# Graph layers 1 to 3 of a four-layer network: the round's order of steps rewritten

## The chip, the cores and the metric

The kernel runs on one core of one Trainium2 chip. The metric is the device time of one execution in microseconds (us). Before the change it is 3620.76 us, the median of three runs (3611.67 to 3627.42). Five engines of the core are named as in the profile: PE is TensorE (PEld its weight loads), DVE is VectorE, ACT is ScalarE, POOL is GpSimd, SP is SyncE, which here only issues transfers.

## The reference

The input is a batch of 64 graphs with 256 nodes and 256 features each (`x`), and a weighted adjacency matrix `adj` for each graph. Four layers follow one another; each is a graph network with a residual sum and a layer norm:

```python
x = _layernorm(x + L0(x, adj))   # a recurrence over the 256 nodes
x = _layernorm(x + L1(x, adj))   # relu(norm_adj @ (x W^T + b))
x = _layernorm(x + L2(x, adj))   # attention, one head of 256, masked by adj
x = _layernorm(x + L3(x, adj))   # attention, 8 heads of 32, masked by adj > 0
```

Layer 0 runs over the nodes for all graphs at once. Layers 1 to 3 treat each graph by itself:

```python
# layer 1
norm_adj = adj_matrix * d_inv_sqrt[:, :, None] * d_inv_sqrt[:, None, :]
output = relu(einsum('bnm,bmo->bno', norm_adj, x @ W.T + b))
# layer 2
att = softmax(scores * mask - NEG * (1.0 - mask))
out = relu((att @ v) @ Wo + bo)
# layer 3, in each of 8 heads of width 32
attn = softmax(where(adj > 0, q @ k.T / sqrt(32), NEG))
out = concat_heads(attn @ v) @ Wo + bo
```

## The kernel before, in words

`_recurrence` does layer 0 and leaves its result in memory. `_layers` (line 850 on) does layers 1 to 3, and it alone is touched. A third function repeats layer 3 in a safer form if a flag asks for it.

In `_layers` each graph is an object whose methods are the steps: a few instructions on one or more engines. All data are 32-bit floats. A tile of one graph is 128 partitions by 2 halves by 256 elements. The steps that the change moves, or that stand around it:

- `xT(l)` transposes the features before layer l: four transposes on PE into one PSUM bank (helper line 930), then one copy by ACT (line 1021).
- `qk2(s)` is a product (eight matmuls, helper line 940) and two ACT activations (1046). `t`, `g`, `v2`, `w2`, `s2`, `f2`, `qk3`, `v3` and `f3` are products too, read out by ACT or DVE. `f2` is read out by three DVE instructions (1087, 1091).
- `s3(hc)` makes the scores of four heads, the half `hc` of the eight. Sixteen matmuls use 32 rows of the array each (1123), into four banks of their own. Then come four DVE adds of the mask (1130) and four ACT exps (1131).
- `o3(hc)` multiplies these by the values: 16 matmuls into 32 columns each, four heads side by side, and 16 with ones in place of the values, which give the sums (1143). DVE then reads out: a reciprocal (1149), a product (1150) and a maximum for the flag (1151). `f3` is the output product, added to `y` by DVE (1158).
- `norm_a(l)` is the first half of a layer norm: five DVE instructions (905 to 908) and one power on POOL (909). `norm_b(l)` is the second half: one DVE instruction (915) and two ACT activations (917).
- `adT` transposes the adjacency matrix: PE, two ACT activations (1011), one DVE comparison (1016). `degrees_a` and `degrees_b` make its degrees on DVE and POOL.
- `store` sends the result out from SP; `load` fetches the three tiles of a graph, also from SP. `bias_3` sends a copy of `y` to memory from SP and adds a bias on POOL.

Nothing reorders the work: a manual schedule is on, and each engine performs its instructions in the order in which the program issues them. That order is the text `ROUND`, seven lines of steps. Five graphs are in work at once, one for each letter: L is being prepared, A is in layer 1, B in layer 2, C in layer 3 and E at layer 3's end. The loop over `t` runs the text once for each round, preceded by the loads of graph t+2, and a graph moves from one letter to the next: what is C in one round is E in the next. Steps of graphs that don't exist are left out in the first and last rounds.

The products and transposes take turns in four PSUM banks (`bank`, line 922). A step that takes a bank waits until the step four turns before has been read out. The four score banks are separate.

Of the kernel before, what the change touches and what calls it, by code (L numbers as in the profile page):

```python
# [849 lines left out]
def _layers(tc, ident, Hd, Yd, x, adj, w1, b1, l2, l3, out):  # L850
# [9 lines left out]
    B, N, D = x.shape  # L860
# [5 lines left out]
    with ExitStack() as ctx:  # L866
# [98 lines left out]
        class Graph:  # L965
# [197 lines left out]


        ROUND = """
            A.xT.1 E.o3.1 B.xT.2 B.qk2.0 C.norm_b.2
            A.t B.qk2.1 B.v2 L.residual_0 B.masks
            E.f3 C.xT.3 A.g C.bias_3 L.norm_a.0
            C.qk3.0 C.qk3.1 E.norm_a.3 A.norm_a.1 L.norm_b.0 B.s2 B.exp2
            C.s3.0 C.v3 B.w2 L.degrees_a  # L1170
            B.pT2 E.norm_b.3 E.store A.norm_b.1 C.s3.1 B.f2 L.degrees_b
            C.o3.0 L.adT B.norm_a.2
        """.split()
        graphs = [Graph(b) for b in range(B)]
        graphs[0].load()
# [129 lines left out]
@with_exitstack  # L1305
def kernel(ctx: ExitStack, tc: tile.TileContext, ins, out):
    nc = tc.nc
    x, adj = ins["x"], ins["adj"]
    B, N, D = x.shape
    main = ctx.enter_context(tc.tile_pool(name="main", bufs=1))  # L1310
    dram = ctx.enter_context(tc.tile_pool(name="dram", bufs=1, space=bass.MemoryType.DRAM))
    ident = main.tile([P, P], F32, name="ident")
    make_identity(nc, ident)
    Hd = dram.tile([N, B, D], F32, name="Hd")
    _recurrence(
        tc, ident, Hd, x, adj,
        *(ins["L0_gnn_" + n] for n in (
            "W_ioux", "b_ioux", "W_iouh", "b_iouh", "W_coux", "b_coux", "W_couh", "b_couh"
        )),
    )  # L1320
    l2, l3 = (
        {w + n: ins[f"{l}_gnn_{w}{n}"] for w in "Wb" for n in "vkqo"} for l in ("L2", "L3")
    )
    Yd = dram.tile([B, P, 2, D], F32, name="Yd")
    found = _layers(tc, ident, Hd, Yd, x, adj, ins["L1_gnn_W"], ins["L1_gnn_b"], l2, l3, out)
    with tc.If(found > 0):
        _layer_3(tc, ident, Yd, adj, l3, out)
# [36 lines left out]
```

## Time and profile before

| what | us |
|---|---|
| median of three runs | 3620.76 |
| lowest and highest | 3611.67, 3627.42 |
| the profiled execution | 3625.61 |
| its span, first to last instruction | 3623.6 |
| PE busy | 3338.4 (92%) |
| DVE busy | 2374.3 (66%) |
| ACT busy | 1836.0 (51%) |
| POOL busy | 1487.7 (41%) |
| mean granted clock of PE | 0.975 |

The profile is one execution. Busy times overlap, since the engines work side by side, and the chain that ended last says which of them set the end: PE has 74% of it. The recurrence takes the first 1592 us or so; the rounds of layers 1 to 3 follow. In the rounds from 1700 to 3500 us PE is busy some 98% of the time, at a granted clock of 1.00. Four views are used below: the page's slices; the windows, which give each engine's busy time and the granted clock in a stretch; the waits, which give the total, the count and the longest of each kind; and the timeline, where a line is a group of like instructions with its start, its length, engine, source line, operation, and in brackets the idle time before it and what ended that.

### The profile page before, as it was taken

The page shows a single profiled execution, that of the slowest core. Times are in us where ns is not written, and L with a number is a line of the kernel's source. Part 1 is how long each engine was busy: PE and PEld are TensorE (multiplying, and loading weights), DVE is VectorE, ACT ScalarE, POOL GpSimd, SP SyncE. Part 2 cuts the span into 40 slices and gives each one's busy share as a digit, 9 for nine tenths or more (in the row PEclk, how much of TensorE's full clock was granted, in tenths as well). Part 3 has the DMA queues.
Part 4 walks back from the last instruction along what each step waited for, and adds up shares of the span by engine and source line. Part 5 has one row for each costly group of instructions (what it writes and reads, how often), then busy time and mean ns, then how long its engine had stood idle before and what let it go on. Part 6 is the DMA issues. An engine that isn't in the chain of part 4 may idle for free.

```text
span 3623.6 us, 81902 instructions
## 1 busy us (share of the span) xinstructions
PE 3338.4 (92%) x30882; PEld 2384.0 (66%) x30882; DVE 2374.3 (66%) x7052; ACT 1836.0 (51%) x4771; POOL 1487.7 (41%) x1669
## 2 busy tenths in 40 slices
PE   5599999999989998858999999999999999999998
PEld 4455555555555555536777777777777777777776
DVE  2366766766667777734777677666677777776765
ACT  0144444444434444424666666666666666666664
POOL 2266666766556777722222222222222222222221
PEclk9799999999999999978999999999999999999999
DMA  8746566687876563240111111111111111111100
GB/s 279 219 129 142 155 170 154 147 189 201 192 186 167 150 165 106 67 107 29 45 45 45 45 45 45 45 45 45 45 45 45 45 45 44 43 45 45 45 27 22
DMA packets 389637, 348.51 MB, mean 96 GB/s; under 512 B 107244, under 2 KB 355192, under 8 KB 384120
## 3 DMA queue, kind: packets, MB, share of 16 engines
q1 hardware_dynamic: 367280, 323.84, 33.6%
q10 hardware_dynamic: 21960, 19.41, 1.6%
q8 instruction: 245, 4.01, 0.5%
q14 instruction: 152, 1.25, 0.1%
HBM read 224.01 MB, written 99.61 MB: 89 GB/s over the span
## 4 chain that ended last, share of the span: by engine, by line
PE 74%; POOL 6%; DMA 6%; DVE 6%; issue 4%; ACT 3%; SPq 2%; ACTq 0%; DVEq 0%; POOLq 0%
PE mm L940 13%; PE o L1143 7%; PE rc L581 4%; PE rc L589 4%; PE s L1123 4%; PE mm_2f L940 3%; PE mm_3v L940 3%; PE mm_3f L940 3%; PE mm_t L940 3%; PE mm_g L940 3%; PE mm_2s L940 3%; PE mm_2v L940 3%; PE mm_2w L940 3%; PE late L505 3%; PE tr_x L930 3%
## 5 line engine op out<-in xcount | busy, mean ns | idle before, releaser
L614 DVE SCALAR_TENSOR_TENSOR ACC<-keep,S,ACC 128x128 f32<-128x128 f32 x1712 | 504.5, 345 | 191.4 <-ACT hs L632 175.8
L909 POOL TENSOR_TENSOR rstd<-rstd,mhalf 128x2 f32<-128x2 f32 x256 | 173.1, 694 | 627.8 <-DVE rstd L908 626.1
L650 POOL TENSOR_TENSOR ACC<-ACC,far 128x384 f32<-128x384 f32 (+1 forms) x313 | 371.9, 1188 | 24.5
L1130 DVE TENSOR_TENSOR p<-s,neg 128x512 f32<-128x512 f32 x512 | 317.7, 683 | 68.6 <-PE s L1123 68.6
L581 PE MATMUL rc<-WxT,xqT 128*64 128x256 f32 x2048 | 329.8, 401 | 1.8 <-issue 1.8
L917 ACT ACTIVATE y<-y,shift,rstd 128x256 f32<-128x256 f32 x512 | 273.5, 598 | 95.3 <-DVE shift L915 91.0
L1035 POOL TENSOR_TENSOR y<-y,g 128x512 f32<-128x512 f32 x64 | 81.2, 1269 | 565.4 <-issue 556.4
L646 POOL TENSOR_TENSOR far<-hs,S 128x384 f32<-128x384 f32 (+1 forms) x313 | 304.8, 974 | 4.7
L1131 ACT ACTIVATE p<-p 128x512 f32<-128x512 f32 x512 | 295.0, 627 | 2.6 <-DVE p L1130 1.6
L752 POOL TENSOR_TENSOR ready<-ACC,dinv 128x128 f32<-128x128 f32 x255 | 102.3, 401 | 419.0 <-DVE ACC L614 397.9
L905 DVE BATCH_NORM_STATS2 st<-y 128x6 f32<-128x256 f32 x512 | 209.1, 408 | 93.8 <-POOL y L1035 89.0
L1158 DVE TENSOR_TENSOR y<-y,mm_3f 128x512 f32<-128x512 f32 x64 | 44.0, 688 | 281.3 <-PE mm_3f L940 281.3
L1149 DVE RECIPROCAL rT<-o 128x256 f32<-128x256 f32 x128 | 224.1, 1751 | 0.3 <-PE o L1143 0.3
L1046 ACT ACTIVATE qk<-mm,b_cols 128x256 f32<-128x256 f32 x256 | 107.4, 470 | 202.6 <-PE mm L940 202.6
L1021 ACT COPY xT<-tr_x 128x512 f32<-128x512 f32 x192 | 112.4, 587 | 182.7 <-PE tr_x L930 182.7
L589 PE MATMUL rc<-WhT,xpT 128*64 128x128 f32 x2048 | 170.2, 287 | 28.1 <-ACT xpT L598 28.0
L598 ACT COPY xpT<-xpT_ps 128x128 f32<-128x128 f32 x256 | 68.3, 267 | 245.5 <-PE xpT_ps L596 245.5
L589 PEld LDWEIGHTS rc<-WhT,xpT 128*64 128x64 f32 x2048 | 107.7, 137 | 117.8 <-ACT xpT L598 84.1
L807 DVE TENSOR_TENSOR zcc<-zc,rc 128x128 f32<-128x128 f32 x256 | 72.8, 284 | 155.1 <-ACT rc L805 155.1
L581 PE MATMUL z_ps<-WxT,xqT 128*64 128x128 f32 x2048 | 171.0, 289 | 0.0
L940 PE MATMUL mm<-xT,W2q 128*128 128x256 f32 x512 | 129.4, 396 | 44.7 <-ACT xT L1021 44.7
L1098 ACT ACTIVATE qk<-mm,b_cols 128x256 f32<-128x256 f32 x256 | 107.5, 471 | 118.2 <-PE mm L940 118.2
(165 smaller groups left out, 7980.2 us busy)
## 6 DMA issues: line engine op xcount, KB each, us to landing
xX<-in_x_dram ACTq DMA_DIRECT2D x16, 1024.0 KB
Us<-xu SPq DMA_DIRECT2D x64, 256.0 KB
rows<-in_adj_dram SPq DMA_DIRECT2D x64, 256.0 KB
ACC<-Us SPq DMA_DIRECT2D x32, 512.0 KB
xq<-in_x_dram SPq DMA_DIRECT2D x64, 256.0 KB
Hw<-hs SPq DMA_DIRECT2D x512, 32.0 KB
Es<-eu SPq DMA_DIRECT2D x64, 256.0 KB
early_sb<-Es SPq DMA_DIRECT2D x32, 512.0 KB
```

The lines of the kernel that those rows point to most:

```text
L581: nc.tensor.matmul(G[o * B:(o + 1) * B], xqT[a, i // 2][:, i % 2, kc, h * B:(h + 1) * B], WxT[:, kc, o, gates], start=False, stop=False, s ...
L589: nc.tensor.matmul(G[o * B:(o + 1) * B], hT[:, kc * B:(kc + 1) * B], WhT[:, kc, o, g], start=False, stop=(kc == 1), skip_group_check=True,)
L614: nc.vector.scalar_tensor_tensor(acc[:, 0, :], keep[:, j % 2, :], s, acc[:, 0, :], ALU.mult, ALU.add)
L646: nc.gpsimd.tensor_mul(tmp[:, 0:count, :], hs.unsqueeze(1).to_broadcast(shape), s.unsqueeze(2).to_broadcast(shape),)
L650: nc.gpsimd.tensor_add(acc, acc, tmp[:, 0:count, :])
L905: nc.vector.bn_stats(st, y[:, c, :])
L917: nc.scalar.activation(y[:, c, :], y[:, c, :], AF.Identity, bias=shift[:, c:c + 1], scale=rstd[:, c:c + 1],)
L940: nc.tensor.matmul(pm[:, c, :], lhsT[:, k, c * P:(c + 1) * P], rhs[:, k, :], start=(k == 0), stop=(k == 1),)
L1130: nc.vector.tensor_add(p, s_ps[i], self.neg3)
L1131: nc.scalar.activation(p, p, AF.Exp, scale=ISQ)
L1143: nc.tensor.matmul(o_ps[i * HD:(i + 1) * HD, part, :], ones if part else self.v3_sb[:, k, h * HD:(h + 1) * HD], self.ps_of[hc][i][:, k, :] ...
L1149: nc.vector.reciprocal(rT, o_ps[:, 1, :])
```

## The change

Only the text `ROUND` is edited; no instruction is added or taken away.

```diff
         ROUND = """
-            A.xT.1 E.o3.1 B.xT.2 B.qk2.0 C.norm_b.2
+            A.xT.1 B.xT.2 B.qk2.0 C.norm_b.2 E.o3.0 E.o3.1
             A.t B.qk2.1 B.v2 L.residual_0 B.masks
-            E.f3 C.xT.3 A.g C.bias_3 L.norm_a.0
-            C.qk3.0 C.qk3.1 E.norm_a.3 A.norm_a.1 L.norm_b.0 B.s2 B.exp2
-            C.s3.0 C.v3 B.w2 L.degrees_a
-            B.pT2 E.norm_b.3 E.store A.norm_b.1 C.s3.1 B.f2 L.degrees_b
-            C.o3.0 L.adT B.norm_a.2
+            C.xT.3 A.g E.f3 C.bias_3 L.norm_a.0
+            C.qk3.0 C.qk3.1 A.norm_a.1 L.norm_b.0 B.s2 B.exp2
+            C.s3.0 C.v3 B.w2 L.degrees_a E.norm_a.3
+            B.pT2 A.norm_b.1 C.s3.1 B.f2 E.norm_b.3 E.store L.degrees_b
+            L.adT B.norm_a.2
         """.split()
```

`o3` of the first half of the heads leaves the last line of one round (as C) and comes into the first line of the next (as E, the same graph), beside `o3` of the second half. The transposes of layer 2 and its first product go ahead of both. `f3` goes behind `xT.3` and `g`. The last norm's first half goes from the fourth line to the end of the fifth, and its second half and the store from behind `pT2` to behind `f2`.

## The prediction

> **What bounds the kernel now.** First the page's forty slices: they separate the recurrence of layer 0 from the rounds of layers 1 to 3 (from slice 18 on), where alone the diff acts.
>
> ```profile
> PE   5599999999989998858999999999999999999998
> ...
> ACT  0144444444434444424666666666666666666664
> ...
> PEclk9799999999999999978999999999999999999999
> ```
>
> TensorE is busy nine tenths or more through the rounds, at the full granted clock; ScalarE has six tenths. The windows view puts numbers on 500 us of it:
>
> ```profile
> core 0: us, PE busy (x) PEld busy (x) DVE busy (x) ACT busy (x) POOL busy (x), PEclk, DMA share, GB/s
> ...
> 2500.00:3000.00 500.00, 489.16 (x3467) 386.83 (x3466) 346.69 (x932) 304.43 (x655) 127.69 (x149) 1.00 0.14 44
> ```
>
> PE 98%, VectorE 69%, ScalarE 61%. The add of g into y (L1035) starts at 2599.39 and, one round later, at 2629.82: a round takes 30.43 us and PE's own order sets it. The averages would let VectorE and ScalarE wait or hurry freely, so the question is what happens at the seam between two rounds. The waits view, 1700 to 3500 us, shows the largest wait of PE and two waits of the others near the seam:
>
> ```profile
> DVE p L1130 <- PE s L1123: 54.7, 59, 0.9
> ...
> PE mm L940 <- ACT xT L1021: 39.8, 59, 0.7
> ACT adT L1011 <- PE tr_ad L930: 30.4, 60, 1.2
> ```
>
> Then the timeline across a seam (start, length of the merged group), ordered by time:
>
> ```profile
> 2608.65 1.15 PE L1123 MATMUL s<-qk,qk 32*128 32x256 f32 x16
> ...
> 2609.55 2.08 ACT L917 ACTIVATE y<-y,shift,rstd 128x256 f32<-128x256 f32 x4
> ...
> 2609.73 1.99 PE L940 MATMUL mm_2f<-w,pT 128*128 128x256 f32 x8
> ...
> 2609.82 2.48 DVE L1130 TENSOR_TENSOR p<-s,neg 128x512 f32<-128x512 f32 x4 [0.93 <-PE s L1123]
> ...
> 2611.53 2.19 ACT L1131 ACTIVATE p<-p 128x512 f32<-128x512 f32 x4
> ...
> 2611.65 1.07 PE L1143 MATMUL o<-p,v 128*32 128x256 f32 x16
> ...
> 2612.22 0.87 DVE L1087 SCALAR_TENSOR_TENSOR f<-mm_2f,sums,b2o_r 128x256 f32<-128x256 f32 x2
> ...
> 2614.21 0.84 ACT L1011 ACTIVATE adT<-tr_ad,dis 128x256 f32<-128x256 f32 x2 [0.50 <-PE tr_ad L930]
> ...
> 2617.10 0.59 ACT L1021 COPY xT<-tr_x 128x512 f32<-128x512 f32 x1 [1.57 <-PE tr_x L930]
> ...
> 2617.74 1.99 PE L940 MATMUL mm<-xT,W2q 128*128 128x256 f32 x8 [0.68 <-ACT xT L1021]
> ```
>
> The reader is to see that ScalarE works without a break from before 2608 to 2613.72, behind PE, and that PE fills that stretch and the next with the two four-wide products (o3, L1143: 2611.65 to 2613.52 and 2614.54 to 2616.41). They are the cover under which ScalarE catches up.
>
> [...] all four norm_b activations sit before the exps at 2611.53, as emitted. [...]every stretch of half clock that can be read lasts a multiple of 3.41 us[...] a product takes 1.72 us from start to start, f2 before the four-wide one 1.92.
>
> The tail of this trace shows what a gap does: 3.11 us of PE waiting, then half clock (stretch, its length, PE busy, granted clock, then DMA).
>
> ```profile
> 3586.00:3587.50 1.50, 0.67 (x2) 1.00 0.00 0
> 3587.50:3589.00 1.50, 0.00 (x0) 1.00 0.00 0
> 3589.00:3590.50 1.50, 0.09 (x1) 0.57 0.00 0
> ...
> 3598.00:3599.50 1.50, 1.50 (x5) 0.52 0.00 0
> ```
>
> ```profile
> 3594.87 3.78 PE L940 MATMUL mm<-xT,W3q 128*128 128x256 f32 x8 [0.68 <-ACT xT L1021]
> ```
>
> The same eight matmuls take 3.78 us there and 1.99 at 2617.74: half clock doubles them.
>
> **The change, part by part**, walked through the seam with the clock of the old trace. Up to s3.1's matmuls (2608.65) PE has the same work.
>
> - *E.norm_a.3 moved behind degrees_a.* Five VectorE instructions (0.43, 0.18, 0.40, 0.18, 0.17 us; 1.3 from first to next) and one pow on POOL, whose queue is idle there. It leaves a stretch where VectorE later waited 0.84 us for s2, gaining nothing, and now stands before the reciprocal of pT2 (2608.60). A.norm_b.1's shift then comes at about 2610.1, s3.1's adds at 2610.1 instead of 2609.82: the 0.93 wait covers all but 0.3. They issue for 2.40 us, to 2612.50.
> - *f2's evictions* keep their place after the adds: 2612.50, the y add from 2613.40, free at 2614.01.
> - *E.norm_b.3 moved behind f2.* Its shift on VectorE is now queued behind f2's evictions: 2614.01 to 2614.18. On ScalarE: A.norm_b.1 2610.2 to 2611.2, s3.1's exps to about 2613.6, then a new wait for that shift to 2614.23, two activations (0.49 each). Queued behind it are adT (2615.2), A's xT copy (2615.95), B's xT copy (2616.42, done 2617.01). adT to xT is 0.73 from start to start, copy to copy 0.47, as in the rows above and at 2608.13 to 2609.07.
> - *B.xT.2 and B.qk2.0 first, o3 behind them.* After f2, PE does three sets of transposes with nothing between: 2611.45 to 2612.95. Then qk2.0 waits for B's xT copy until 2617.06: a gap of 4.1 us, where it was 0.7. The two o3, ready since 2613.6, stand behind qk2.0.
> - *Both o3 side by side.* qk2.0 to o3.0 takes 1.92, o3.0 to o3.1 1.75 (the tail shows such a pair, 3582.24 to 3583.99), o3.1 to t 1.87. So t starts at 2617.06 + 5.54 = 2622.60; it was 2619.57. **Plus 3.03 us a round**[...].
> - *f3 behind g, store later.* PE's sum is the same. VectorE: o3's two evictions (2.6 us each, the reciprocal 1.75 of it) end 9.1 us after qk2.0's start, t's add at 9.8; g stands at 11.2: 1.3 us of cover. f3's add ends about 4.5 us before s2's mask product: covered. On SP the store comes after norm_b.3, with three loads behind it; those loads are first used a round later. Nothing.
> - *The clock.* [...] the half clock comes in every round. [...] mean **2.4 us a round**. No other engine hides it, since PE's order sets the round.
>
> Sum: 3.03 + 2.4 = 5.4 us a round. The seams with all five graphs present are 60, with partial ones 61: 331 us. The profiled execution took 3625.6 us (span 3623.6), which gives 3957; the median shown is 3620.8, 4.8 below it, which gives 3952.
>
> Unknown costs: half clock on the four-wide products is not in the trace. If they are not slowed at all, a round loses about 1.2 less[...]. I take plain doubling, as for the 128-wide products. The walk itself may be off by 0.4 us a round. That gives 3.8 to 7.5 us a round, 3853 to 4078.
>
> **Rivals.**
> (a) *The gap without the clock*: PE waits as walked[...] Time: 3620.8 + 61 x 3.03 = 3806.
> (b) *The other side: ScalarE is not late at the seam[...].* Place: qk2.0's wait for B's xT copy. If norm_b.3 were through before adT's transposes end (2611.7), adT and the two copies would end at 2613.6 and t would start at 2619.2: 0.38 less a round, 3598. It decides from the copy's end: before 2614.0 the round gains, after it loses. For it: ScalarE is only 61% busy. Against: four exps cannot start before s3.1's adds, and end at 2613.6 with three more steps behind them.
> (c) *Half clock twice*: [...] 1.7 us more: 4056.
>
> **How the numbers follow.** Forecast 0.72, (a) 0.12, (b) 0.08, (c) 0.08. A measurement tells about 0.5% from no change. Slower by more: 0.91; within: 0.02; faster: 0.07, both from (b). The range leaves out (b) and the far end of (c): 3795 to 4050; the forecast's own is 3853 to 4050.
>
> **What would show it.** PE's wait for ACT xT before q of layer 2 near 4 us in each round; ACT y L917 waiting for DVE shift about 0.6 us there; PEclk near 0.93 in the 500 us windows (half clock for some 5 us of 36) instead of 1.00; a round of about 36 us; s3.1's adds without their wait for PE. It is wrong if that wait stays under 1.5 us, or if PEclk stays 1.00.

## The result and the profile after

The changed kernel takes 3929.32 us, the median of four runs (3922.35 to 3933.2); the kernel before, run beside it, takes 3617.95 (3611.67 to 3627.42). The ratio is 1.0847, with a 95% interval of 1.0829 to 1.0866. The profiled execution took 3933.2 us, its span 3931.4. The forecast was 3952, with a range from 3795 to 4050.

The slices of the page after:

```profile
PE   5599999998899988498888988898889888898888
...
ACT  0244444444444444254555445554555455545554
...
PEclk9799999999999999799999999999999999999999
```

In the recurrence, up to slice 17, little has changed. From there on most of PE's nines have become eights and ACT's sixes fives and fours. The clock row still shows nines, since a nine covers all from 0.9. The windows view, with two more digits:

```profile
core 0: us, PE busy (x) PEld busy (x) DVE busy (x) ACT busy (x) POOL busy (x), PEclk, DMA share, GB/s
...
2500.00:3000.00 500.00, 445.55 (x2982) 347.62 (x2981) 313.04 (x809) 256.76 (x562) 110.95 (x129) 0.93 0.12 38
```

In the same 500 us PE does 2982 matmuls where it did 3467, at a mean clock of 0.93 where it was 1.00. The start of the add of g into y, from one round to the next, gives the round. Its mean between 2400 and 2900 us is 35.49 us; before, it was 30.43. That is 5.05 us a round, and 308 us if 61 rounds lose as much. From the first of these starts to the last, the two traces themselves differ by 304.0 us, and their spans by 307.8: the loss lies in the rounds.

The waits view after, 1750 to 3800 us (total, times, longest):

```profile
PE mm L940 <- ACT xT L1021: 225.2, 58, 3.9
...
DVE neg L1016 <- ACT adT L1011: 104.9, 58, 1.8
ACT y L917 <- DVE shift L915: 72.1, 116, 0.8
```

PE's wait for the copy of xT has grown from 0.7 to 3.9 us in each round. The wait of VectorE's s3 adds for PE, first of the three shown of before, has left the list: VectorE now reaches them later, when the scores are there already. The seam between two rounds, in the timeline after:

```profile
2615.49 1.15 PE L1123 MATMUL s<-qk,qk 32*128 32x256 f32 x16
...
2616.84 2.48 DVE L1130 TENSOR_TENSOR p<-s,neg 128x512 f32<-128x512 f32 x4
...
2617.96 2.18 ACT L1131 ACTIVATE p<-p 128x512 f32<-128x512 f32 x4
...
2618.83 1.04 PE L930 MATMUL tr_x<-ident,y 128*128 128x128 f32 x8
...
2620.14 0.69 DVE L1091 SCALAR_TENSOR_TENSOR y<-f,y 128x512 f32<-128x512 f32 x1
2620.75 0.15 DVE L915 SCALAR_TENSOR_TENSOR shift<-mv,rstd 128x2 f32<-128x2 f32 x1
...
2620.94 1.09 ACT L917 ACTIVATE y<-y,shift,rstd 128x256 f32<-128x256 f32 x2 [0.80 <-DVE shift L915]
2621.94 0.81 ACT L1011 ACTIVATE adT<-tr_ad,dis 128x256 f32<-128x256 f32 x2
...
2622.65 1.06 ACT L1021 COPY xT<-tr_x 128x512 f32<-128x512 f32 x2
...
2623.77 3.78 PE L940 MATMUL mm<-xT,W2q 128*128 128x256 f32 x8 [3.90 <-ACT xT L1021]
...
2627.48 1.94 PE L1143 MATMUL o<-p,v 128*32 128x256 f32 x16
...
2629.18 1.43 PE L1143 MATMUL o<-p,ones 128*32 128x256 f32 x16
...
2632.27 1.99 PE L940 MATMUL mm_t<-W1T,xT 128*128 128x256 f32 x8
```

Read it from the end. Layer 2's q waited 3.90 us for two copies. These stood behind adT, adT behind the last norm's activations, and those behind the exps and a wait of 0.80 for VectorE, which came to the shift (L915) only at 2620.75, behind the three read-outs of f2. PE had finished its transposes at 2619.87. When it starts again, eight matmuls take 3.78 us instead of 1.99. Three windows laid on the gap and on what follows it show the clock:

```profile
2619.90:2623.70 3.80, 0.00 (x0) 0.00 (x0) 1.96 (x6) 3.00 (x7) 0.00 (x0) 0.93 0.20 65
2623.80:2630.20 6.40, 6.40 (x36) 3.79 (x40) 2.06 (x6) 1.81 (x4) 2.53 (x3) 0.52 0.43 125
2630.30:2636.00 5.70, 5.70 (x57) 4.21 (x50) 5.17 (x9) 0.00 (x0) 0.00 (x0) 1.00 0.12 44
```

PE is fully busy in the second window, yet at a mean clock of 0.52: what is lost there doesn't show as idle time.

### The profile page after: what moved, and what is told of

Its sections match the earlier page's. It is cut to its first block, busy times and chain, and to the rows that moved or that the text cites. A ratio compares the mean times of both kernels' runs of the same rounds, so it can differ in the third digit from the quotient of the medians.

```text
span 3931.4 us, 81900 instructions
## 1 busy us (share of the span) xinstructions
PE 3442.5 (88%) x30882; PEld 2448.7 (62%) x30882; DVE 2426.7 (62%) x7052; ACT 1815.5 (46%) x4771; POOL 1494.3 (38%) x1669
## 4 chain that ended last, share of the span: by engine, by line
PE 58%; DVE 20%; issue 6%; DMA 6%; ACT 5%; POOL 4%; SPq 1%; ACTq 0%; DVEq 0%; POOLq 0%
PE mm L940 14%; DVE p L1130 7%; PE o L1143 6%; PE rc L581 4%; PE rc L589 4%; PE mm_t L940 3%; PE mm_3f L940 3%; PE mm_2s L940 3%; PE mm_g L940 3%; PE mm_2v L940 3%; PE late L505 3%; DVE ACC L614 2%; PE z_ps L581 2%; ACT xT L1021 2%; PE z_ps L589 2%
## 5 line engine op out<-in xcount | busy, mean ns | idle before, releaser
L940 PE MATMUL mm<-xT,W2q 128*128 128x256 f32 x512 | 225.4, 618 | 242.1 <-ACT xT L1021 242.1
L940 PEld LDWEIGHTS mm<-xT,W2q 128*128 128x128 f32 x512 | 152.0, 310 | 289.0 <-ACT xT L1021 257.4
L1000 POOL TENSOR_TENSOR dis<-dis,mhalf 128x2 f32<-128x2 f32 x64 | 44.2, 691 | 376.5 <-DVE dis L999 376.5
```

The lines of the kernel that those rows point to most:

```text
L940: nc.tensor.matmul(pm[:, c, :], lhsT[:, k, c * P:(c + 1) * P], rhs[:, k, :], start=(k == 0), stop=(k == 1),)
```

## The experiments

Eight kernels were run. All times are medians, and each ratio is to runs of the kernel before beside it. The clock and the rounds (means between 2400 and 2900 us) are those of one traced execution each.

**Both o3 ahead of layer 2's transposes.** The changed kernel with one line edited:

```diff
-            A.xT.1 B.xT.2 B.qk2.0 C.norm_b.2 E.o3.0 E.o3.1
+            A.xT.1 E.o3.0 E.o3.1 B.xT.2 B.qk2.0 C.norm_b.2
```

> The changed kernel with one edit: both o3 go ahead of layer 2's transposes and q in the first line; all else as changed. Theory (PE has no cover while ScalarE catches up at the seam; the gap then halves the clock): the two o3 are the cover again, PE's wait before q of layer 2 falls from 3.9 us to about 0.7, the granted clock in the rounds is 1.00, and t starts about 0.3 us later than before: 3636 us (3600 to 3660). Rival (the loss comes from the moved end of layer 3, or from the two o3 standing side by side with their readouts 5.2 us on VectorE): it stays near 3930.

Measured: 3626.23 us, ratio 1.0012 (0.9998 to 1.0025), a round of 30.52 us. The clock is 1.00 from 2000 to 3000 us. PE's waits, 1750 to 3400 us:

```profile
PE mm L940 <- ACT xT L1021: 36.5, 54, 0.7
...
PE tr_x L930 <- ACT xT L1021: 18.1, 53, 0.3
```

Everything else of the change is in this kernel, the side-by-side o3 and the moved end included, and the loss is gone. So without the new place of the o3, behind q of layer 2 and not ahead of its transposes, the rest of the change costs nothing that can be measured. What it adds where the o3 have that place is the next question.

**The end of layer 3 put back.** Again the changed kernel, with lines 4 to 6 as before the change:

```diff
-            C.qk3.0 C.qk3.1 A.norm_a.1 L.norm_b.0 B.s2 B.exp2
-            C.s3.0 C.v3 B.w2 L.degrees_a E.norm_a.3
-            B.pT2 A.norm_b.1 C.s3.1 B.f2 E.norm_b.3 E.store L.degrees_b
+            C.qk3.0 C.qk3.1 E.norm_a.3 A.norm_a.1 L.norm_b.0 B.s2 B.exp2
+            C.s3.0 C.v3 B.w2 L.degrees_a
+            B.pT2 E.norm_b.3 E.store A.norm_b.1 C.s3.1 B.f2 L.degrees_b
```

> The changed kernel with the last norm's two halves and the store put back where they were before (lines 4 to 6 as before); first line as changed. Theory: ScalarE ends B's xT copy 1.3 us earlier, PE's gap before q of layer 2 is 2.8 us, which still halves the clock in about four rounds of five; 1.7 us a round from the walk and about 1.7 from the clock: 3828 us (3770 to 3870). Rival (the moved end is the whole cause): 3618. Rival (the gap counts, the clock doesn't): 3724.

Measured: 3824.09 us, ratio 1.0567 (1.055 to 1.0585), a round of 33.82 us. In its PE timeline:

```profile
2606.79 1.15 PE L1123 MATMUL s<-qk,qk 32*128 32x256 f32 x16
...
2613.96 2.55 PE L940 MATMUL mm<-xT,W2q 128*128 128x256 f32 x8 [2.79 <-ACT xT L1021]
2616.44 1.94 PE L1143 MATMUL o<-p,v 128*32 128x256 f32 x16
```

From s3.1 to q is 7.17 us, 1.11 less than in the changed kernel (8.28): that is what the moved end adds to the gap. A gap of 2.8 us remains, and so does most of the half clock. In 60 rounds with all graphs present, 53 have a stretch of half clock of 3.41 us and seven have none, more than the four in five that were expected; in the changed kernel 36 have one of 3.41 us and 24 one of 6.83. With its longer gap and longer half clock, the moved end makes about a third of the loss (105 of 311 us), but only behind the other cause: the next kernel has it alone.

**The end of layer 3 moved, nothing else.** The kernel before with lines 3 to 6 as in the change:

```diff
-            E.f3 C.xT.3 A.g C.bias_3 L.norm_a.0
-            C.qk3.0 C.qk3.1 E.norm_a.3 A.norm_a.1 L.norm_b.0 B.s2 B.exp2
-            C.s3.0 C.v3 B.w2 L.degrees_a
-            B.pT2 E.norm_b.3 E.store A.norm_b.1 C.s3.1 B.f2 L.degrees_b
+            C.xT.3 A.g E.f3 C.bias_3 L.norm_a.0
+            C.qk3.0 C.qk3.1 A.norm_a.1 L.norm_b.0 B.s2 B.exp2
+            C.s3.0 C.v3 B.w2 L.degrees_a E.norm_a.3
+            B.pT2 A.norm_b.1 C.s3.1 B.f2 E.norm_b.3 E.store L.degrees_b
```

> The kernel before with only layer 3's end moved back (f3, both halves of the last norm, store as in the change); o3 stays where it was. Theory: ScalarE is as late as in the changed kernel, but the o3 of each half covers it; o3.0's bank comes free 0.4 us later, so at most 0.45 us a round: 3618 to 3650. Clock 1.00. Rival (the moved end is the cause): near 3930.

Measured: 3624.26 us, ratio 1.0009 (0.9999 to 1.0018), a round of 30.52 us. The waits of this kernel, 1750 to 3400 us, show the same longest wait of 0.8 us on ScalarE for the shift as after the change, and no more on PE than before:

```profile
ACT y L917 <- DVE shift L915: 102.2, 162, 0.8
...
PE mm L940 <- ACT xT L1021: 36.4, 54, 0.7
```

So the moved end costs 1.67 us a round without a cover (35.49 less 33.82, of which 1.11 is the longer gap), and 0.09 with it (30.52 less 30.43).

**Filling the gap, first try.** A method `warm(n)` issues n matmuls of two constant weights into one bank, which nothing reads:

```diff
+            def warm(self, n):
+
+                pm = bank(f"warm_{self.b}")
+                for _ in range(n):
+                    nc.tensor.matmul(
+                        pm[:, 0, :], W2["q"][:, 0, 0:P], W2["k"][:, 0, :], start=True, stop=True
+                    )
...
-            A.xT.1 B.xT.2 B.qk2.0 C.norm_b.2 E.o3.0 E.o3.1
+            A.xT.1 B.xT.2 B.warm.12 B.qk2.0 C.norm_b.2 E.o3.0 E.o3.1
```

> The changed kernel with work added: twelve matmuls of 128x256, which nothing reads, stand between layer 2's transposes and its q. They take 2.6 us of PE, inside the gap of 3.9. Theory (part of the loss is the half clock that the gap brings): q of layer 2 starts at the same place, the gap left is about 1 us, the clock stays 1.00, and the time FALLS to 3806 us (3790 to 3830). Rival (the gap alone is the loss): the time stays at 3929. Rival (PE is the bound whatever the gap): 2.6 us a round more, 4090.

Measured: 3906.76 us, ratio 1.0799 (1.0781 to 1.0817), with the clock at 1.00 and a round of 34.98 us. The expectation missed by 100 us, and the PE timeline of this kernel shows why:

```profile
2609.37 5.45 PE L986 MATMUL warm<-W2k,W2q 128*128 128x256 f32 x24 [0.28 <-DVE f L1095]
...
2614.65 1.89 PE L940 MATMUL mm<-xT,W2q 128*128 128x256 f32 x8
```

Twelve calls are 24 instructions and 5.45 us, so the filler no longer fits: the copy is done at 2612.92, q starts 1.7 us later. Even so a round of the kernel with more work in it is 0.5 us shorter than one of the changed kernel. The next two runs have other sizes of the filler.

**Filling the gap with half of that, and with next to nothing.** The same kernel with six calls, then with one.

> The changed kernel with six matmul calls (twelve instructions, 2.6 us of PE; a call of this type is two instructions, which the run with twelve calls showed: 5.45 us, so that there q of layer 2 came 1.7 us late) added in the gap, read by nothing. Theory (half clock is a part of the loss): q of layer 2 starts where it does in the changed kernel, the granted clock is 1.00, a round takes 33.3 us, the time is 3800 us (3785 to 3815). Rival (the gap alone is the loss): 3929.

> The changed kernel with one such call (two instructions, 0.43 us) added at the same place, read by nothing; the banks take turns as in the run with six. Theory: the gap stays over 3 us, the clock is halved as in the changed kernel, 3925 us (3900 to 3945). Rival (the six calls help by shifting the turn of the banks): near 3800.

Measured with six: 3799.35 us, ratio 1.047 (1.0448 to 1.0492), a round of 33.40 us. With one: 3929.79 us, ratio 1.0832 (1.0814 to 1.085), a round of 35.49 us, the same as the changed kernel. The seam with six calls, in the PE timeline:

```profile
2622.35 1.15 PE L1131 MATMUL s<-qk,qk 32*128 32x256 f32 x16
...
2627.02 2.86 PE L986 MATMUL warm<-W2k,W2q 128*128 128x256 f32 x12 [0.28 <-DVE f L1095]
2630.62 1.99 PE L940 MATMUL mm<-xT,W2q 128*128 128x256 f32 x8 [0.74 <-ACT xT L1029]
2632.54 1.07 PE L1151 MATMUL o<-p,v 128*32 128x256 f32 x16
...
2636.13 2.00 PE L940 MATMUL mm_t<-W1T,xT 128*128 128x256 f32 x8
```

From s3.1 to q is 8.27 us, as in the changed kernel (8.28): the filler delays nothing. But q takes 1.99 us and not 3.78. The two windows, first with six calls, then with one:

```profile
2500.00:3000.00 500.00, 484.63 (x3352) 386.50 (x3344) 332.17 (x856) 274.93 (x598) 116.24 (x136) 1.00 0.13 40
```

```profile
2500.00:3000.00 500.00, 455.43 (x3010) 351.46 (x3008) 311.37 (x802) 257.36 (x565) 109.99 (x128) 0.93 0.12 38
```

Useless work makes the changed kernel 130 us faster, and only through the clock; the control with one call, which shifts the banks' turns in the same way, changes nothing. This splits the loss. Of 5.05 us a round, 33.40 - 30.43 = 2.97 are the gap with the o3 behind it and all else that was moved, and 35.49 - 33.40 = 2.09 are the half clock.

**A step that is ready, put into the wait.** From the kernel before, layer 1's product t goes ahead of q of layer 2. The first half of C's norm goes behind o3.1, which is meant to let VectorE free o3's bank sooner.

```diff
-            A.xT.1 E.o3.1 B.xT.2 B.qk2.0 C.norm_b.2
-            A.t B.qk2.1 B.v2 L.residual_0 B.masks
+            A.xT.1 E.o3.1 C.norm_a.2 B.xT.2 A.t B.qk2.0 C.norm_b.2
+            B.qk2.1 B.v2 L.residual_0 B.masks
...
-            C.o3.0 L.adT B.norm_a.2
+            C.o3.0 L.adT
```

> From the kernel before: layer 1's product t goes between layer 2's transposes and q, and the first half of C's norm behind o3.1. Theory (a step ready to run is what the seam needs): t covers the wait for B's xT copy, PE's wait of 0.7 to 0.9 us a round goes, a round takes 29.7 us: 3573 us (3560 to 3595). Rival (VectorE's readout of o3 holds the banks, and the wait only moves to layer 2's k): 3605 to 3625.

Measured: 3560.46 us, ratio 0.9814 (0.9797 to 0.9831), a round of 29.47 us. It is 1.9% faster than the kernel before. Of the 0.96 us that a round gains, 0.68 is the wait at q, which is gone. The two moves were not tried apart, so what each is worth stays open. The PE timeline has no wait left at this place:

```profile
2617.76 0.66 PE L930 MATMUL tr_x<-ident,y 128*128 128x128 f32 x4
2618.25 1.89 PE L940 MATMUL mm_t<-W1T,xT 128*128 128x256 f32 x8
2619.98 1.89 PE L940 MATMUL mm<-xT,W2q 128*128 128x256 f32 x8
```

**The same with both o3 side by side.** As the last, with `E.o3.0` ahead of `E.o3.1` in the first line and `C.o3.0` gone from the last.

> As the last, and both o3 stand side by side ahead of layer 2's transposes. Theory: [...] 3560 us (3545 to 3595). Rival: two o3 readouts in a row (5.2 us of VectorE) hold the banks until layer 2's q and k: 3605 to 3640.

Measured: 3562.6 us, ratio 0.9827 (0.9806 to 0.9848), a round of 29.52 us. This is the time of the one before; the 13 us by which it was expected below that one (3560 against 3573) aren't there. Its waits, 1750 to 3400 us, show a small one of PE's loads that the kernel before it doesn't have:

```profile
PEld mm_g L940 <- ACT qk L1046: 16.5, 54, 0.3
```

That is no less than the 13 us. That it ate up the gain is an argument from the trace, and not shown: no run removed it.

## Why the prediction was right

Point by point, in its own order:

- *E.norm_a.3 on VectorE*: the adds of s3.1 were to come 1.45 us after that product's first matmul; measured 1.35 (2615.49 to 2616.84), with no wait of their own.
- *E.norm_b.3 behind f2*: the new wait of ScalarE for its shift was put at 0.6 us. It is 0.80, and ScalarE's queue behind it is the one named: adT, then two copies.
- *The gap*: 4.1 us forecast, 3.90 measured. From s3.1 to q 8.41 forecast, 8.28 measured.
- *q to t through both o3*: 5.54 us forecast, 5.51 measured where the clock is full (2630.62 to 2636.13). So the walk's 3.03 us a round stands against 2.97. At the seam itself the filled kernel needs 13.78 us from s3.1 to t, and the kernel before 10.92 (2608.65 to 2619.57): 2.86 of the 2.97 lie there.
- *The clock*: half clock in each of 60 rounds, as forecast. That four-wide products are slowed like the others was assumed there, and it held: the first half of o3.0 takes 1.70 us from start to start (2627.48 to 2629.18), where it took 0.89 (2611.65 to 2612.54). In this round, one with a half clock of 6.83 us, q to t takes 8.50 us, 2.99 more than at full clock. The size of the loss, the author's estimate, was put a little high: 2.4 us against 2.09. Rounds with 6.83 us of half clock, 24 of the 60, take about 36.4 us and those with 3.41 about 34.9, so 3.0 and 1.5 above the filled kernel.
- *f3 and the store at nothing*: the kernel with the moved end alone is at 1.0009, so they cost at most 0.2% with all else that was moved there.

The 23 us between 3952 and 3929 are nearly all the clock's and the walk's excess: 61 rounds by 5.43 - 5.05, of which the clock's part is 0.3 us and the walk's 0.06. Rival (a), the gap without the clock, gave 3806, and the kernel that has just that runs at 3799. Rival (b) needed ScalarE on time at the seam. Its idle share was real, but it lay elsewhere in the round: in the kernel after, 550.5 us over 58 rounds, or 9.5 us in each, are spent waiting to read out q and k of layer 2. Rival (c) asked for a longer half clock than was found.

One expectation was wrong in size: the filler of twelve calls, because a call is two instructions here. The code and the lines of before could have said so: a product is four calls and shows as x8. Two others were right in time, but not in all they said: with the end put back, half clock came in more rounds than expected, and the side-by-side o3 brought no gain.

## What to carry to other kernels

Before a step is moved ahead of another in one engine's order, ask what covered the first one's wait. Here a product that was ready stood in front of one that wasn't, and swapping them made a wait of 0.7 us one of 3.9, which no busy share of the kernel before announced. The gap was paid twice here: 2.97 us a round with the clock at 1.00, and 2.09 more for the half clock that followed it. In the changed order even useless matmuls in the gap were worth more than rest: they saved 130 us where they ended before the wait did, and 23 us where they ended after it. The better mending is the last but one experiment: put a step that is ready into the wait. It was tried on the kernel before, whose wait was 0.7 us.

## What the runs showed that was not expected

- The changed kernel's rounds do not vary freely. Between 2400 and 2900 us they take 34.7 to 35.1 us or 36.1 to 36.5, and from one start of half clock to the next it is always 34.1 or 37.5 us. The control with one call repeats the mean round to 0.01 us, and the counts, 36 short and 24 long. So it isn't chance. What sets their turns was not tried.
- Which gaps the half clock followed, over the runs: with PE's wait before q of layer 2 at 3.9 us (the changed kernel) it came in 60 of 60 rounds, with 2.8 us (the end put back) in 53 of 60. With one filler call the waits are 0.29 and 2.90 us with 0.70 us of work between them, and the mean clock from 2500 to 3000 us is 0.93, as in the changed kernel. With six calls they are 0.28 and 0.74 us with 2.86 us of work between, and the clock is 1.00. It is 1.00 too where the wait is 0.7 us: in the kernel before, with both o3 ahead, and with the moved end alone. What sets apart the seven rounds without half clock was not shown.
- VectorE's comparison for the mask of layer 3 (L1016) waits in each round for ScalarE's adT (L1011), 1.8 us in the changed kernel. Both only read the same transposed bank. Why it waits was not tried, and nothing on the path waited for it.
